# Two transformer layers on one core: attention's last masks, layer 1's first input sums, and where a product stands in two units

## The chip, the core and the metric

The kernel runs on one core of a Trainium2 chip. A core has five engines with a queue each: TensorE (matrix products; PE in the profile, its weight loads PEld), VectorE (DVE), ScalarE (ACT), GpSimd (POOL) and SyncE (SP), which starts transfers between the chip's large memory and SBUF, the on-chip memory of 128 partitions. TensorE writes its results to PSUM, which VectorE and ScalarE can read. Engines run on their own and wait for each other where a result or a buffer is needed; within one engine's queue the order is fixed when the program is compiled. The metric is the device time of one execution, in microseconds (us).

## What is computed

The input `x` has 2 sequences of 1024 rows of 512 numbers. Each of two layers normalises the rows and adds an "attention" branch and a feed-forward branch, both computed from the same normalised rows:

```python
xn = _layernorm(x, axis=-1)
x = x + _L0_attn_ref(xn, ...) + _L0_ffn_ref(xn, W1, W2, W3)
xn = _layernorm(x, axis=-1)
x = x + _L1_attn_ref(xn, W_qkv, b_qkv, W_out, b_out) + _L1_ffn_ref(xn, w_gate, w_up, w_down)
```

The change lies in layer 1. Its attention is causal, with 16 heads of 32 numbers, and its feed-forward keeps the two largest of each four hidden numbers:

```python
scores = jnp.einsum('bqhe,bkhe->bhqk', q, k) * scale
scores = jnp.where(causal[None, None], scores, -jnp.inf)
attn = jax.nn.softmax(scores, axis=-1)
...
h = jax.nn.silu(jnp.einsum('bsh,hi->bsi', x, w_gate)) * jnp.einsum('bsh,hi->bsi', x, w_up)
h_sparse = _sparsify_2to4(h)
return jnp.einsum('bsi,ih->bsh', h_sparse, w_down)
```

All of it is in float32.

## The kernel before

The 2048 rows are held as four blocks of 512 (`TT`), transposed: `xt1[i]` has the 512 features as 4 chunks of 128 partitions, and 512 columns, one for each row. Layer 0 runs first, then layer 1's attention, then layer 1's feed-forward.

**Attention** works through 8 units, each one sequence (of 2) and a group of 4 heads. A unit has two halves `j` of 512 queries. For a half, the key blocks `kt` of 128 come one after another: 4 for the first half, 8 for the second, so 12 steps a unit and 96 in all (`second`). A step's `weights` (line 1086) forms the scores of 4 heads on TensorE in two PSUM tiles, adds minus the row maxima to them by small products, and takes the exponential on ScalarE into two SBUF tiles `pt` (for `kt` 0 it is called `acc`). Where a key block lies on the diagonal (`kt >= 4 * j`), 128 of the columns hold entries that the mask forbids; a GpSimd `affine_select` (line 1117) sets these to zero. `gather` (line 1126), one step later, multiplies the values by `pt` into the bank `o` (line 1137) and adds `pt` to `acc` (line 1145), whose column sums are the softmax's denominators: `total` (line 1152) forms these on TensorE, `divide` (line 1164) takes reciprocals on VectorE and multiplies on GpSimd (line 1169). The additions of line 1145 go to GpSimd, and to VectorE once no maxima are left to be found:

```python
eng = nc.vector if per * u + 4 * j + kt + ahead >= len(second) else nc.gpsimd
```

`per` is 12, `ahead` 13 and `len(second)` 96, so this holds from step 83 on: the last step of unit 6 and all of unit 7.

The **order of the steps** is written out: a loop over steps `n` from -13 to 95 calls, in this order, `weights` of step n, what `put_mid` has for n, `gather` of step n-1, what `put_after` has, the search for maxima of step n+13, one part of a projection (`one_part`, chosen by due time), and what `put` has for n (`what_is_fixed`). `in_program_order` (line 48) ties each engine's instructions of this loop to that order. A last loop after it works off what is left: the output projections `project_out(8)` to `project_out(15)` (line 1176), each of two parts, 4 products that end in one VectorE addition to `x` (line 1179), with `total` and `divide` of the last half between them. The projections use two PSUM banks by turns. This last loop is not tied: the scheduler that compiles the program orders it.

**Layer 1's feed-forward** has 16 units; two make a group. A unit forms gate and up of a quarter of hidden features for two blocks of rows `x` and `y`, in `gate_up` (line 186), by Strassen's scheme as Winograd has it: seven products in place of eight, at the price of sums of the inputs (`tt`, four of them, by `combine_x` on VectorE, lines 156 to 161; one overwrites half of `y`) and of the weights (`s`, by `combine_w` on GpSimd, lines 169 to 172). Each product (`products`, line 175) is 4 matmuls of 128x128 by 512 columns, two for each half `m` of its pair of PSUM banks. Four of them add up in `pa`, two in `pc`, one stands alone in `pb`. After each product into `pa` that is not the last, ScalarE copies `pa` as it stands (lines 208, 216, 222), since the sum so far is wanted, and the next product into `pa` has to wait for that copy. `other_half` (line 201) is the product into `pb`, with a VectorE addition to `e[0]`. In units 1 to 15 it comes between the products with `s[1]` and `s[2]`; in unit 0 (`first`) it comes second, and the input sums are made by `hook(0)` right before it. From unit 2 on, the thinning (`sparsify`) and down products (`down_by_seven`) of the group before are put between the products, by the hooks. From line 1336 on the order is written out and tied as in attention.

Of the kernel before, what the change touches and what calls it, by code (L numbers as in the profile page):

```python
# [12 lines left out]
ALU = mybir.AluOpType  # L13
# [22 lines left out]
def two_layers(ctx: ExitStack, tc: tile.TileContext, t: dict, out: bass.AP):  # L36
# [135 lines left out]
        nc.gpsimd.tensor_sub(s[3], w1[:, :, 2:, :], s[1])  # L172
        return s

    def products(pair, a, x, start=False, stop=False):

        for m in range(2):
            for k in range(2):
                nc.tensor.matmul(  # L179
                    pair[:, m, :], a[:, m, k, :], x[:, k, :],  # L180
                    start=start and k == 0, stop=stop and k == 1, skip_group_check=True,
                )

    turns = 0

    def gate_up(pool, name, w1, w2, s, x, y, tt, h, hook, first=None):


        nonlocal turns
        e = [pool.tile([P, 2, TT], F32, tag=f"e{m}", name=f"e{m}_{name}") for m in range(1, 4)]  # L190

        pa, pc = (ps_pair(f"p{m}_{name}", (turns + m) % 3) for m in (0, 2))
        turns += 1

        def silu(m, i, gate):
            nc.scalar.activation(h(m, i), gate, AF.Silu)

        def up(m, i, lin):
            nc.vector.tensor_mul(h(m, i), h(m, i), lin)

        def other_half():
            pb = ps_pair(f"p1_{name}", turns % 3)
            products(pb, w1[:, :, 2:, :], x[:, 2:, :], start=True, stop=True)
            nc.vector.tensor_add(e[0], e[0], pb)
            hook(3)

        products(pa, w1[:, :, :2, :], x[:, :2, :], start=True)
        nc.scalar.copy(e[0], pa)
        hook(0)
        if first:  # L210
            other_half()
            y, tt = first()
        products(pc, s[0], tt[0], start=True)
        hook(1)
        products(pa, s[1], tt[1])
        nc.scalar.copy(e[1], pa)
        hook(2)
        if not first:
            other_half()
        products(pa, s[2], tt[2])  # L220

        nc.scalar.copy(e[2], pa)
        silu(0, 0, e[0][:, 0, :])
        nc.vector.tensor_add(e[2], e[2], pc)  # L224
        up(0, 0, e[0][:, 1, :])
        hook(4)
        silu(1, 1, e[2][:, 0, :])
        products(pa, w2[:, :, 2:, :], tt[3], stop=True)
        silu(1, 0, pa[:, 0, :])
        up(1, 1, e[2][:, 1, :])  # L230
        hook(5)
        up(1, 0, pa[:, 1, :])
        products(pc, s[3], y[:, 2:, :], stop=True)
        nc.vector.tensor_add(e[1], e[1], pc)
        hook(6)
        silu(0, 1, e[1][:, 0, :])
        up(0, 1, e[1][:, 1, :])
# [664 lines left out]
    in_program_order(start0)  # L902


    first_gu = {}
    with tc.tile_pool(name="b", bufs=1, reuse_waits="tile") as b:

        qk = {
# [13 lines left out]
        nc.gpsimd.affine_select(  # L922
            out=mask, in_=mask, compare_op=ALU.is_ge, fill=MASKED,
            base=0, pattern=[[-1, P]], channel_multiplier=1,
        )
        identb = b.tile([P, P], BF16, name="identb")
        nc.vector.tensor_copy(identb, ident)
# [146 lines left out]
        def shift_rows(u, half):  # L1074
# [8 lines left out]
            negs[u, half] = b.tile([P, TT], BF16, tag="neg", name=f"neg_{u}_{half}", bufs=4)  # L1083
            nc.vector.tensor_copy(negs[u, half], px[:, :NJ].rearrange("p t c -> p (t c)"))

        def weights(u, j, kt):

            q, k, neg = qk[u, 0], qk[u, 1], negs[u, j]
            name = f"{u}_{j}_{kt}"
            s = max(0, kt - 4 * j) * P  # L1090
            cols = slice(j * 512 + s, (j + 1) * 512)
            pair = [ps_wide(f"s_{name}_{p}") for p in range(2)]
            for h in range(4):
                rows = slice(h * HD, (h + 1) * HD)
                nc.tensor.matmul(  # L1095
                    pair[h // 2][:, h % 2, s:], k[rows, kt * P : (kt + 1) * P], q[rows, cols],
                    start=True, stop=False,
                )
            for h in range(4):
                rows = slice(h * HD, h * HD + 3)  # L1100
                nc.tensor.matmul(  # L1101
                    pair[h // 2][:, h % 2, s:], onesb[rows, :], neg[rows, s:],
                    start=False, stop=True,
                )
            got = []
            for p in range(2):

                if kt == 0:
                    pt = b.tile([P, 2, 512], F32, tag=f"acc{p}", name=f"acc_{name}_{p}", bufs=2)
                else:  # L1110
                    pt = b.tile([P, 2, 512], F32, tag="pt", name=f"pt_{name}_{p}", bufs=5)
                nc.scalar.activation(  # L1112
                    pt[:, :, s:], pair[p][:, :, s:], AF.Exp, scale=1.0 / math.sqrt(HD)
                )
                if kt >= 4 * j:
                    d = pt[:, :, s : s + P]
                    nc.gpsimd.affine_select(  # L1117
                        out=d, in_=d, compare_op=ALU.is_ge, fill=0.0,
                        base=0, pattern=[[0, 2], [1, P]], channel_multiplier=-1,
                    )  # L1120
                got.append(pt)
            return u, j, kt, s, got

        held, sums = {}, {}

        def gather(u, j, kt, s, pts):

            bb, hg = units[u]
            if kt == 0:
                held[u, j] = ps_bank(f"o_{u}_{j}", 0)  # L1130
                sums[u, j] = pts
            po = held[u, j]
            last = kt == 4 * j + 3
            v = vals[bb, kt // NJ, kt % NJ][:, hg * P : (hg + 1) * P]
# [4 lines left out]
                    start=(kt == 0), stop=last, tile_position=(0, h * HD),  # L1139
                )  # L1140
            if kt:

                eng = nc.vector if per * u + 4 * j + kt + ahead >= len(second) else nc.gpsimd
                for acc, pt in zip(sums[u, j], pts):
                    eng.tensor_add(acc[:, :, s:], acc[:, :, s:], pt[:, :, s:])  # L1145
            if last:
                att[u, j] = b.tile([P, 512], F32, tag="att", name=f"att_{u}_{j}", bufs=12)
# [4 lines left out]
        def total(u, j):  # L1152

            pw = ps_wide(f"w_{u}_{j}")[:, 0, :]
            for h in range(4):
                rows = slice(h * HD, (h + 1) * HD)
                nc.tensor.matmul(  # L1157
                    pw[rows, :], ones, sums[u, j][h // 2][:, h % 2, :],
                    start=True, stop=True, tile_position=(0, h * HD),
                )  # L1160
            inv[u, j] = b.tile([P, 512], F32, tag="inv", name=f"inv_{u}_{j}", bufs=1)
# [159 lines left out]
        n = len(second)  # L1321
        for m in range(QT, QT + NJ):
            rest.append((n, n + 9, project_out(m)))
        while rest or open_parts or fixed:
            one_part(n)
            what_is_fixed(n)
# [9 lines left out]
    with tc.tile_pool(name="c", bufs=1, reuse_waits="tile") as c_:  # L1336
# [167 lines left out]
                    if half == 0:  # L1504
                        tail.append((some_steps, n, 1, (3, 3, 3, 2)[2 * j + i]))

        tt, next_tt, second = None, None, None
        s_of = {}

        def unit_sums(n):  # L1510
# [2 lines left out]
        for n, (pb, g, half) in enumerate(units):  # L1513
# [11 lines left out]

            def hook(at):
                nonlocal tt, next_tt, second
                if n == at == 0:
                    tt, *make = combine_x(c_, x, y, "c0")
                    for f in make:  # L1530
                        f()
                for f, *args in between1.pop((n, at), ()):
                    f(*args)
                if at == 5 and n + 1 < len(units):
# [1 line left out]
                if at == 5 and n % 2 == 0 and n:  # L1536
                    load_down(n // 2)
                if at == 5 and n == len(units) // 2 - 1:
                    next_tt, first, second = combine_x(c_, xt1[2], xt1[3], "c1")
                    first()  # L1540

            gate_up(
                c_, f"c{n}", gu_w.pop((n, 0)), gu_w.pop((n, 1)), s_of.pop(n), x, y, tt,
                lambda m, i: h[:, 2 * half + m, i, :], hook,
                (lambda: (y, tt)) if n == 0 else None,
            )
            if n + 2 < len(units):
                load_gu(n + 2)
# [77 lines left out]
```

## Time and profile before

| what | us |
|---|---|
| median of 3 runs | 1851.51 |
| the three runs | 1851.51, 1851.51, 1860.42 |
| the profiled execution | 1851.87 |
| its span, first to last instruction | 1850.1 |
| layer 0 ends, attention's projections start | 676.45 |
| attention's last unit starts (scores of step 84) | 1177 |
| output projections 8 to 15 start | 1214.99 |
| layer 1's feed-forward starts | 1243.75 |

| engine | busy us | share of the span |
|---|---|---|
| TensorE | 1794.7 | 97% |
| VectorE | 1124.7 | 61% |
| GpSimd | 819.6 | 44% |
| ScalarE | 478.5 | 26% |

A timeline row is one engine's run of equal instructions: start, length, engine, line, operation, output and inputs by the program's names, shape and count, and in brackets the idle time before it with what ended it. Rows of a float32 product count two records for each matmul. In the table of stretches a number in brackets is a count of instructions. The granted TensorE clock is 0.996 over the run.

### The profile page before, as it was taken

The numbers are of one execution on the slowest core, as the hardware profiler recorded it, in microseconds if no ns is written. First come the engines' busy times: TensorE is split into PE (matmuls) and PEld (weight loads), VectorE is DVE, ScalarE is ACT, GpSimd is POOL, SyncE is SP. The second block draws the span as 40 slices with busy tenths as digits, with TensorE's granted clock in tenths as the row PEclk, the third lists the DMA queues.
The fourth block names the chain that finished last, engine by engine and source line by source line (L and its number), as shares of the span: only waits on it lengthen the run. The fifth ranks groups of instructions, "written<-read, shape, count | busy, mean of one in ns | idle before, by whom it ended". The sixth has DMA issues, their size and how long they took to land.

```text
span 1850.1 us, 18897 instructions
## 1 busy us (share of the span) xinstructions
PE 1794.7 (97%) x7348; PEld 916.4 (50%) x7348; DVE 1124.7 (61%) x1464; ACT 478.5 (26%) x683; POOL 819.6 (44%) x711
## 2 busy tenths in 40 slices
PE   7999999999999999999999999999999999999998
PEld 4446566555555564333333333333455555555553
DVE  3685444556544438566666566752867778668654
ACT  2322222222221102334343443412212212211210
POOL 4335364256542222467666766623243343334300
PEclk9999999999999999999999999999999999999999
DMA  6121111011101100000001000011011112201101
GB/s 228 35 80 34 35 35 46 23 46 35 35 23 34 35 18 12 1 12 13 12 1 35 12 13 1 24 46 42 27 57 34 46 32 72 80 23 57 34 1 46
DMA packets 29465, 68.12 MB, mean 37 GB/s; under 512 B 3392, under 2 KB 11584, under 8 KB 27840
## 3 DMA queue, kind: packets, MB, share of 16 engines
q1 hardware_dynamic: 28656, 66.61, 11.1%
q8 instruction: 59, 0.97, 0.2%
q10 hardware_dynamic: 720, 0.30, 0.1%
q14 instruction: 30, 0.25, 0.0%
HBM read 62.70 MB, written 4.19 MB: 36 GB/s over the span
## 4 chain that ended last, share of the span: by engine, by line
PE 87%; DVE 5%; POOL 3%; ACT 2%; issue 2%; DMA 0%; SPq 0%; ACTq 0%; POOLq 0%; DVEq 0%
PE p_a L179 20%; PE p_c L179 19%; PE d L297 19%; PE pq L990 6%; PE m L1042 4%; PE s L1095 4%; PE o L1137 3%; PE po L990 3%; PE pv L990 3%; PE dr L1454 2%; POOL acc L1145 2%; PE w L1157 1%; DVE tops L1050 1%; PE pp L579 1%; PE s L1101 1%
## 5 line engine op out<-in xcount | busy, mean ns | idle before, releaser
L315 POOL TENSOR_TENSOR x<-x,de 128x512 f32<-128x512 f32 x87 | 125.4, 1456 | 297.3 <-DVE x L310 162.5
L1145 POOL TENSOR_TENSOR acc<-acc,pt 128x1024 f32<-128x1024 f32 (+3 forms) x138 | 233.6, 1717 | 0.0
L1050 DVE TENSOR_REDUCE tops<-m 128x2 f32<-128x1024 f32 (+2 forms) x192 | 180.8, 955 | 49.1 <-PE m L1042 44.6
L310 DVE TENSOR_TENSOR x<-x,d 128x512 f32<-128x512 f32 x145 | 99.2, 684 | 151.5 <-PE d L297 150.5
L1112 ACT ACTIVATE pt<-s 128x1024 f32<-128x1024 f32 (+3 forms) x160 | 115.1, 766 | 180.1 <-PE s L1101 166.9
L297 PE MATMUL d<-td,h 128*128 128x256 f32 x592 | 139.9, 380 | 2.2 <-DVE h L272 2.2
L297 PEld LDWEIGHTS d<-td,h 128*128 128x128 f32 x592 | 112.2, 190 | 46.2 <-issue 29.2
L990 PE MATMUL pq<-xt,wqk 128*128 128x512 f32 x256 | 124.5, 614 | 0.8 <-ACT qk L1006 0.8
L179 PE MATMUL p_a<-t_a,s_a 128*128 128x512 f32 x256 | 116.9, 600 | 2.0 <-DVE t_a L156 2.0
L179 PE MATMUL p_c<-xt,s_c 128*128 128x512 f32 x256 | 115.2, 593 | 2.5 <-DVE e_c L224 1.4
L179 PE MATMUL p_a<-xt,w 128*128 128x512 f32 x256 | 116.8, 599 | 0.7 <-ACT xt L136 0.7
L179 PE MATMUL p_a<-xt,s_a 128*128 128x512 f32 x256 | 116.6, 598 | 0.0
L179 PE MATMUL p_c<-xt,gu 128*128 128x512 f32 x256 | 114.9, 592 | 0.0
L179 PE MATMUL p_c<-t_c,s_c 128*128 128x512 f32 x256 | 114.6, 592 | 0.0
L1049 DVE TENSOR_TENSOR m<-m,mask 128x256 f32<-128x256 f32 x128 | 54.7, 427 | 97.3 <-PE m L1042 92.7
L1042 PE MATMUL m<-qk,qk 32*128 32x512 f32 (+3 forms) x768 | 107.2, 533 | 3.7 <-ACT acc L1112 3.0
L1095 PE MATMUL s<-qk,qk 32*128 32x512 f32 (+3 forms) x768 | 93.5, 532 | 3.1 <-ACT pt L1112 2.2
L172 POOL TENSOR_TENSOR s_c<-gu,s_c 128x512 f32<-128x512 f32 x16 | 20.4, 1275 | 134.2 <-PE p_c L179 134.2
L1117 POOL TENSOR_SCALAR_AFFINE_SELECT pt<-pt 128x256 f32<-128x256 f32 x112 | 48.3, 448 | 69.5 <-ACT pt L1112 68.9
L990 PEld LDWEIGHTS pq<-xt,wqk 128*128 128x128 f32 x256 | 44.2, 189 | 65.9 <-issue 61.8
L179 PEld LDWEIGHTS p_a<-xt,s_a 128*128 128x128 f32 x256 | 47.2, 190 | 57.1 <-issue 56.7
L179 PEld LDWEIGHTS p_c<-xt,s_c 128*128 128x128 f32 x256 | 48.5, 190 | 54.2 <-issue 52.9
(240 smaller groups left out, 3044.6 us busy)
## 6 DMA issues: line engine op xcount, KB each, us to landing
w<-in_W SPq DMA_DIRECT2D x32, 512.0 KB, 3.6
gu<-in_gu SPq DMA_DIRECT2D x32, 512.0 KB, 3.5
wd<-in_down SPq DMA_DIRECT2D x8, 1024.0 KB, 4.8
x<-in_x SPq DMA_DIRECT2D x16, 256.0 KB, 4.3
w2h<-in_W2q SPq DMA_DIRECT2D x4, 1024.0 KB, 11.5
xr<-in_x SPq DMA_DIRECT2D x16, 256.0 KB, 2.7
wqk<-in_WqkvT SPq DMA_DIRECT2D x16, 256.0 KB, 3.1
out_x<-x SPq DMA_DIRECT2D x16, 256.0 KB, 2.0
```

Of the source, the lines that this page charges most:

```text
L179: nc.tensor.matmul(pair[:, m, :], a[:, m, k, :], x[:, k, :], start=start and k == 0, stop=stop and k == 1, skip_group_check=True,)
L297: nc.tensor.matmul(out_[:, j, :], lhs[:, q, j * P : (j + 1) * P], rhs[:, q], start=m in (0, 1, 3, 4) and j == q == 0, stop=j == q == 1, sk ...
L310: nc.vector.tensor_add(r, r, out_)
L315: nc.gpsimd.tensor_add(r, r, u2[half])
L990: nc.tensor.matmul(got[0], lhs(k), rhs(k), start=(k == 0), stop=(k == KC - 1))
L1042: nc.tensor.matmul(pair[h // 2][:, h % 2, :e], q[rows, qt * P : (qt + 1) * P], k[rows, c * 512 : c * 512 + e], start=True, stop=True,)
L1049: nc.vector.tensor_add(d, d, mask.unsqueeze(1).to_broadcast([P, 2, P]))
L1050: nc.vector.tensor_reduce(out=tops[u][:, c, qt, 2 * p : 2 * p + 2], in_=pair[p][:, :, :e], axis=mybir.AxisListType.X, op=ALU.max,)
L1095: nc.tensor.matmul(pair[h // 2][:, h % 2, s:], k[rows, kt * P : (kt + 1) * P], q[rows, cols], start=True, stop=False,)
L1112: nc.scalar.activation(pt[:, :, s:], pair[p][:, :, s:], AF.Exp, scale=1.0 / math.sqrt(HD))
L1137: nc.tensor.matmul(po[rows, s:], v[:, rows], pts[h // 2][:, h % 2, s:], start=(kt == 0), stop=last, tile_position=(0, h * HD),)
L1145: eng.tensor_add(acc[:, :, s:], acc[:, :, s:], pt[:, :, s:])
```

## The change

It has three parts.

*Masks.* The test by which line 1145 chooses its engine becomes a function, `idle_vector`. Where it holds for the step before (steps 84 to 95, all of unit 7), the mask on the diagonal is no longer a GpSimd `affine_select` but a VectorE minimum of `pt` with a new constant tile `allowed`, which is 1e30 where the mask allows and 0 elsewhere. `allowed` is made by two GpSimd instructions at the start of attention.

*Input sums.* A pool `sums`, opened before attention's pool and kept to the end, holds `t1`, `t2` and `t4`. The four sums for the first pair of blocks are put at `n + 5` and `n + 6` of the last loop of attention (`n` is 96), and unit 0's hook no longer makes them. The dictionary that was named `sums` is now `sums_of`.

*The product.* `products` takes the halves `m` that it is to do. In units 0 and 1 (`split`) `other_half` does `m = 0` between the products with `s[1]` and `s[2]`, and `m = 1`, with the addition to `e[0]` and hook 3, after the product with `s[2]` and its copy. Unit 0 has no special order any more.

```diff
+        pb = None
+
+        def other_half(of=(0, 1)):
+            nonlocal pb
+            if 0 in of:
+                pb = ps_pair(f"p1_{name}", turns % 3)
+            products(pb, w1[:, :, 2:, :], x[:, 2:, :], start=True, stop=True, of=of)
+            if 1 in of:
+                nc.vector.tensor_add(e[0], e[0], pb)
+                hook(3)
...
         if not first:
-            other_half()
+            other_half((0,) if split else (0, 1))
         products(pa, s[2], tt[2])
 
         nc.scalar.copy(e[2], pa)
+        if split:
+            other_half((1,))
         silu(0, 0, e[0][:, 0, :])
...
+    sums = ctx.enter_context(tc.tile_pool(name="sums", bufs=1))
     with tc.tile_pool(name="b", bufs=1, reuse_waits="tile") as b:
...
+        allowed = b.tile([P, P], F32, name="allowed")
+        nc.gpsimd.memset(allowed, -MASKED)
+        nc.gpsimd.affine_select(
+            out=allowed, in_=allowed, compare_op=ALU.is_ge, fill=0.0,
+            base=0, pattern=[[1, P]], channel_multiplier=-1,
+        )
...
+        def idle_vector(u, j, kt):
+
+            return per * u + 4 * j + kt + ahead >= len(second)
+
...
-                if kt >= 4 * j:
-                    d = pt[:, :, s : s + P]
+                d = pt[:, :, s : s + P]
+                if kt >= 4 * j and idle_vector(u, j, kt - 1):
+                    nc.vector.tensor_tensor(
+                        d, d, allowed.unsqueeze(1).to_broadcast([P, 2, P]), ALU.min
+                    )
+                elif kt >= 4 * j:
                     nc.gpsimd.affine_select(
...
-                eng = nc.vector if per * u + 4 * j + kt + ahead >= len(second) else nc.gpsimd
-                for acc, pt in zip(sums[u, j], pts):
+                eng = nc.vector if idle_vector(u, j, kt) else nc.gpsimd
+                for acc, pt in zip(sums_of[u, j], pts):
...
+        first_tt, *make = combine_x(sums, xt1[0], xt1[1], "c0")
+        for m, f in enumerate(make):
+            put(n + 5 + m, f)
         while rest or open_parts or fixed:
...
-        tt, next_tt, second = None, None, None
+        tt, next_tt, second = first_tt, None, None
...
-                if n == at == 0:
-                    tt, *make = combine_x(c_, x, y, "c0")
-                    for f in make:
-                        f()
...
-                    next_tt, first, second = combine_x(c_, xt1[2], xt1[3], "c1")
+                    next_tt, first, second = combine_x(sums, xt1[2], xt1[3], "c1")
...
-                lambda m, i: h[:, 2 * half + m, i, :], hook,
-                (lambda: (y, tt)) if n == 0 else None,
+                lambda m, i: h[:, 2 * half + m, i, :], hook, split=n < 2,
             )
```

## The prediction

> **What bounds the kernel now.** I read the page first. The busy times and the chain that ended last say that TensorE sets the end almost everywhere:
>
> ```profile
> PE 1794.7 (97%) x7348; PEld 916.4 (50%) x7348; DVE 1124.7 (61%) x1464; ACT 478.5 (26%) x683; POOL 819.6 (44%) x711
> ...
> PE 87%; DVE 5%; POOL 3%; ACT 2%; issue 2%; DMA 0%; SPq 0%; ACTq 0%; POOLq 0%; DVEq 0%
> ```
>
> So an edit is worth the TensorE idle time that it takes away or makes. I looked for that idle time in the timeline around the edited places: the last unit of attention (1176 to 1215 us), the last output projections (1215 to 1244) and the first two units of layer 1's feed-forward (1244 to 1299). TensorE's rows of layer 1, with the idle time in brackets:
>
> ```profile
> 1243.75 7.03 PE L179 MATMUL p_c<-xt,gu 128*128 128x512 f32 x16
> 1250.62 7.03 PE L179 MATMUL p_c<-t_c,s_c 128*128 128x512 f32 x16
> 1258.79 3.67 PE L179 MATMUL p_c<-xt,s_c 128*128 128x512 f32 x8 [1.15 <-issue]
> 1263.57 3.70 PE L179 MATMUL p_c<-t_c,gu 128*128 128x512 f32 x8 [1.10 <-ACT e_c L222]
> ...
> 1288.97 3.70 PE L179 MATMUL p_c<-t_c,gu 128*128 128x512 f32 x8 [1.10 <-ACT e_c L222]
> ```
>
> A product is 8 records, 3.43 us. TensorE stops three times in two units, each time because ScalarE is copying the accumulator (1.01 us) that the next product adds to: 1.15 + 1.10 + 1.10 = 3.35 us. Nothing stops it from 1215 to 1257.65, so the projections and the input sums cost it nothing today. In attention's last unit:
>
> ```profile
> 1181.89 1.59 PE L1137 MATMUL o<-acc,v 128*32 128x512 f32 x8 [1.26 <-POOL acc L1117]
> ...
> 1202.83 1.05 PE L1137 MATMUL o<-pt,v 128*32 128x512 f32 x4 [0.43 <-POOL pt L1117]
> ...
> 1204.17 1.05 PE L1137 MATMUL o<-pt,v 128*32 128x512 f32 x4 [0.29 <-POOL pt L1117]
> ...
> 1210.97 0.98 PE L1137 MATMUL o<-pt,v 128*32 128x256 f32 x8 [1.81 <-POOL pt L1117]
> ```
>
> With another 0.37 at 1186.1 the masks on GpSimd cost 1.26 + 0.37 + 0.43 + 0.29 + 1.81 = 4.16 us of idle TensorE. That is the most that moving them can give. But their new engine is the busiest after TensorE there, as the busy time by stretch shows (columns: stretch, its length, then PE, PEld, DVE, ACT, POOL):
>
> ```profile
> 1176.00:1190.00 14.00, 12.30 (x111) 4.48 (x113) 8.16 (x11) 7.24 (x15) 10.67 (x16) 1.00 0.13 53
> ...
> 1200.00:1215.00 15.00, 12.48 (x93) 3.99 (x87) 13.89 (x15) 5.78 (x9) 8.33 (x9) 1.00 0.32 119
> ```
>
> VectorE has 1.1 us free in the last 15. Its queue and GpSimd's there:
>
> ```profile
> 1201.35 2.50 DVE L1145 TENSOR_TENSOR acc<-acc,pt 128x1024 f32<-128x1024 f32 x2
> 1203.77 0.94 DVE L1167 RECIPROCAL inv<-inv 128x128 f32<-128x128 f32 x1
> 1204.63 2.41 DVE L1145 TENSOR_TENSOR acc<-acc,pt 128x1024 f32<-128x1024 f32 x2
> 1206.96 0.94 DVE L1167 RECIPROCAL inv<-inv 128x128 f32<-128x128 f32 x1
> 1207.83 2.82 DVE L1145 TENSOR_TENSOR acc<-acc,pt 128x768 f32<-128x768 f32 x2
> ```
>
> ```profile
> 1201.40 3.43 POOL L1117 TENSOR_SCALAR_AFFINE_SELECT pt<-pt 128x256 f32<-128x256 f32 x4 [7.31 <-ACT pt L1112]
> 1207.99 1.85 POOL L1169 TENSOR_TENSOR att<-att,inv 128x512 f32<-128x512 f32 x1 [3.16 <-DVE inv L1167]
> 1209.79 3.10 POOL L1117 TENSOR_SCALAR_AFFINE_SELECT pt<-pt 128x256 f32<-128x256 f32 x4
> ```
>
> The two engines hold each other up: a select is 0.40 us alone and 1.37 beside VectorE's additions (two of the four at 1201.40), the multiplication 1.27 alone and 1.85 there.
>
> **The change, part by part. 1: the product taken apart.** In units 0 and 1 half of `other_half` (1.72 us) comes before the product with `s[2]`, half after it. Each half lies over a copy: 1.01 us, started 0.2 after the product's end, is done 1.2 us after it, under 1.72. All three stops go: **-3.35 us**. What becomes late: the addition to `e[0]` now runs after the second half, 17.4 to 18.6 us into the unit, so the first silu follows at 18.6 and the addition to `e[2]` ends at 19.7. The last product needs that at 20.6: 0.9 us of slack. Unit 0's activation table load (1.28) fits between copy and silu. Vector work of unit 1 ends as late after its last product as before, so the two stops at 1313 to 1316 (0.29 + 1.50, the thinning steps on VectorE) stay. Bounds: 0 to -3.35; I take the whole, since the cover is longer than the copy in the same trace.
>
> **2: the input sums.** Four VectorE additions of 1.22 us (1244.56 to 1249.3) leave unit 0. Unit 0's second product now wants the first sum at 1247.2, where before `other_half` lay between. They go to the loop behind attention, two at a time, 2.4 us each. That loop is not held to the written order, and their inputs are old: the scheduler may put three of them as early as 677.5, where VectorE idles 15.06 us, and the in-place one into mid-attention. At the written place an addition of a projection (0.69) could wait 2.4 us; 2.4 + 0.69 = 3.1, and its bank is wanted after 3.43. So nothing either way; if all four come in a row, 4.9 + 0.7 - 3.4 = 2.2. I take **0**, bounds 0 and +2.2. No transfer moves with them. The 12 KB of `sums` push attention's tiles up, so that two of its first loads may wait for other tiles: the value weights on SP's queue (issued 608.9, landed 5.2 later, wanted at 711.1) and the bias on ScalarE's (653.8). Issued at 672, when layer 0's last GpSimd addition ends, the first lands 34 us early, and ScalarE is idle until 680.1 anyway: nothing. The tile `allowed` costs GpSimd 0.20 + 0.29 us near 672, before VectorE's mask is wanted at 692.6: nothing.
>
> **3: the masks.** Sixteen selects leave GpSimd, sixteen minima of 128x256 join VectorE, all in the last unit. Nearest row: the addition of 128x256 at 1190.3, 0.36 us, the next starting 0.28 after it; the addition of `mask` from PSUM is 0.43. I take 0.30 a piece, bounds 0.28 and 0.62 (such an addition beside GpSimd at 1181.5). Each minimum waits for its exponential on ScalarE, and the order puts it ahead of the step before's additions to `acc`: behind it queue these, the reciprocals, the copy of `neg`; TensorE waits for the minimum and, at the unit's end, for `acc`.
>
> I walked VectorE's queue through with these durations. First half (key steps 0 to 3): GpSimd's last additions run until 1181.3, the second minimum gets in after them, and the output product that started at 1181.89 starts at 1180.6 and is through 0.9 us earlier. But the additions of step 1, run at 1183.1 today, now stand behind the minima of step 2 and start at 1184.8; the copy of `neg` comes at 1188.1 against 1188.3, and TensorE's row that waits for it gains only 0.5. Second half (4 to 7), all 0.5 earlier at first: the reciprocals end at 1200.9, step 4's minima run at 1200.9 and, behind the second exponential, 1201.8; its product gains 1.7. Then come two additions (2.3), a reciprocal (0.9) and only then, at 1205.1, step 5's minima: that product starts 0.4 earlier than its 1205.91. Step 6's minima come behind two more additions and a reciprocal, and the second behind GpSimd's multiplication, at 1210.3; step 7's at 1212.2; the last additions end at 1214.5, and the addition that frees the first projection's bank at 1215.1 where it was 1214.6. TensorE restarts at about 1215.2 against 1214.99: **+0.2 us**. So the masks' 4.16 us of stops are not won: VectorE gets 8 x 0.30 = 2.4 us more in a stretch with 1.1 free, and wins back about 1 us of contention with the selects. Bounds: -4.16 (all stops gone) and, with 0.62 for each of those eight, 5.0 - 1.1 - 1.0 = +2.9.
>
> [...]
>
> **Sum.** -3.35 + 0 + 0.2 = -3.15 us. The profiled execution took 1851.87 (span 1850.1 and 1.77 around it): 1848.7. The median of the runs is 0.36 below it: **1848.4 us**, 0.17% faster. A measurement of this kernel tells about 0.5% (9.3 us) from no change, so this is no change.
>
> **Rivals.**
> - *The masks' stops go too.* VectorE's order leaves the minima early enough, and 4.16 us come back. For it: GpSimd is named in all five stops. Against: 13.89 of 15 us busy. 1851.5 - 3.35 - 4.16 = 1844.0.
> - *VectorE becomes the bound, and the kernel slower.* The place is steps 5 to 7 of the last unit, where each pair of minima stands behind up to 3.2 us of additions and reciprocal. At 0.62 a minimum the stretch grows by 2.9; it decides once the masks' part costs over 3.35, that is from 0.68 a piece or one more addition of 1.2 ahead of the last `acc`. At 0.9 a piece (half-way to the 1.47 of the contended one): 7.2 - 2.1 = 5.1, and 1851.5 - 3.35 + 5.1 = 1853.3. For it: contended additions of 0.62 to 1.47. Against: GpSimd has little left to contend with.
> - *The sums stand in the way.* All four in a row among the projections' additions: +2.2, 1850.6. For it: nothing fixes their place. Against: they are ready hundreds of us before.
> - *Taking apart does nothing*, because the copy or the silu now ends last: 1851.7. Against: 1.2 under 1.72.
>
> **How the numbers follow.** Chances: forecast 0.60 (own range 1846.5 to 1850), masks won 0.12, VectorE bound 0.12, sums 0.09, nothing 0.07. The range takes in the second case and reaches to the edge of the third: 1844.0 to 1853.0, with little over 0.1 left out. None of them reaches 9.3 us. Faster by over 0.5% would need more than all stops named here (7.5); slower by it would need the third case doubled, or the runs near 1860.42 that the kernel before has once in three. So 0.02, 0.94, 0.04.
>
> **What would show it.** Right: no idle TensorE before the products with `s[2]` and `tt[3]` in units 0 and 1, so that these two units take 3.35 us less; no GpSimd selects after 1179; VectorE over 14 of the last 15 us of attention, and output products waiting for VectorE's minima around steps 5 and 6 instead of GpSimd's selects; the first projection behind attention within 1 us of 1215.0. Wrong: that projection at 1212 or 1218; stops before the products with `s[0]` in unit 0, for a sum not made; additions of the projections late enough to hold a bank.

## The result and the profile after

| | median us | lowest to highest | executions | ratio to before, 95% interval |
|---|---|---|---|---|
| before | 1856.12 | 1851.19 to 1862.93 | 22 | |
| after | 1850.01 | 1847.47 to 1854.98 | 22 | 0.9972 [0.9964, 0.9981] |

The changed kernel is 0.28% faster by the means of its executions (1850.84 us against 1855.97), under the 0.5% that was called no change, and its median of 1850.01 us lies in the forecast range of 1844.0 to 1853.0 us. The forecast time, 1848.4, is 1.6 us too low although the forecast gain, 0.17%, is too small: it started from a median of three executions, 1851.51 us, and over 22 the kernel before has 1856.12. From there the same gain would have given 1853.0 us, 3.0 too high, so that the time itself was met this closely is luck in part.

The profiled execution of after took 1854.98 us (span 1853.3), more than before's profiled one (1851.87). One execution of each can't be compared as a whole, because TensorE's granted clock falls to a half for some stretches of 3.4 or 6.8 us, and their number and places differ: three in before's (from 28.7, 1813.9 and 1831.0 us), five in after's (from 31.8, 76.2, 1195.8, 1817.0 and 1834.1). Each execution has its mean clock on record, so below a *time at full clock* is given as well: the time less (1 - mean clock) x time. It is an estimate: the clock is on record to three digits, which is 0.9 us either way for one execution, and it takes off as much where TensorE waits as where it works. Before's 29 executions beside the first experiments spread by 2.4 us (standard deviation) and by 0.75 at full clock; they have a mean of 1844.4 us by it and after's 22 one of 1839.7; both have about 11 us taken off. One execution of an experiment below, the profiled one of neg_scalar, had a granted clock of 0.95 in every 20 us from 1180 to 1260 too and took 1913.16 us; it is left out of that kernel's ratio and times, and only its stops are read.

The page of after:

```profile
PE 1801.9 (97%) x7348; PEld 918.7 (50%) x7348; DVE 1136.3 (61%) x1480; ACT 479.1 (26%) x683; POOL 810.3 (44%) x697
...
PE 88%; DVE 6%; ACT 2%; POOL 2%; issue 2%; DMA 1%; ACTq 0%; DVEq 0%; POOLq 0%
```

VectorE has 16 instructions more, GpSimd 14 less (16 selects gone, two to make `allowed`). In the chain VectorE rose from 5% to 6% and GpSimd fell from 3% to 2%. TensorE's timeline in the first two units of the feed-forward (start, length, engine, line, operation, tiles, shape, count):

```profile
1261.33 1.88 PE L179 MATMUL p_c<-xt,gu 128*128 128x512 f32 x4
1263.04 3.60 PE L179 MATMUL p_c<-xt,s_c 128*128 128x512 f32 x8
1266.48 1.88 PE L179 MATMUL p_c<-xt,gu 128*128 128x512 f32 x4
1268.19 3.60 PE L179 MATMUL p_c<-t_c,gu 128*128 128x512 f32 x8
...
1275.06 3.60 PE L179 MATMUL p_c<-xt,gu 128*128 128x512 f32 x8
...
1287.08 3.60 PE L179 MATMUL p_c<-xt,s_c 128*128 128x512 f32 x8
...
1292.23 3.60 PE L179 MATMUL p_c<-t_c,gu 128*128 128x512 f32 x8
...
1299.09 3.60 PE L179 MATMUL p_c<-xt,gu 128*128 128x512 f32 x8
```

The product appears in two halves of 4 records, one on each side of the product with `s[2]`. Unit 1 runs from 1275.06 to 1299.09, where unit 2 starts. No row of the two units has an idle time in brackets: the three stops of 1.15, 1.10 and 1.10 us are gone. In attention's last unit they are not gone but have other causes (TensorE's timeline of after):

```profile
1185.52 1.81 PE L1162 MATMUL o<-acc,v 128*32 128x512 f32 x8 [0.42 <-ACT att L1172]
1193.72 0.40 PE L1122 MATMUL s<-neg,onesb 3*128 3x512 bf16 x4 [0.65 <-DVE neg L1101]
1213.42 1.17 PE L1162 MATMUL o<-pt,v 128*32 128x384 f32 x8 [1.60 <-DVE pt L1138]
1217.16 0.63 PE L1162 MATMUL o<-pt,v 128*32 128x256 f32 x4 [0.17 <-DVE pt L1138]
1218.57 0.63 PE L1162 MATMUL o<-pt,v 128*32 128x256 f32 x4 [0.79 <-DVE pt L1138]
1221.40 1.13 PE L179 MATMUL p_c<-xt,gu 128*128 128x512 f32 x2
1223.12 5.42 PE L1007 MATMUL po<-wout,att 128*128 128x512 f32 x12 [0.59 <-DVE x L1203]
```

The bracketed times add up to 4.22 us; before had 4.16. GpSimd's selects were named in all five before; now VectorE is named in five of six: the copy of `neg`, the minima (line 1138), the addition that frees a bank (line 1203). The row at 1221.40 was not expected: two records of unit 0's first product, placed ahead of the first output projection behind attention. The stretches that answer to the two shown of before (its length, then PE, PEld, DVE, ACT, POOL):

```profile
1180.50:1194.50 14.00, 12.86 (x117) 4.62 (x115) 10.10 (x19) 7.40 (x15) 6.05 (x8) 1.00 0.14 55
1208.12:1223.12 15.00, 11.85 (x86) 3.85 (x79) 14.51 (x22) 5.54 (x9) 1.27 (x1) 1.00 0.33 126
```

In the last 15 us ahead of that projection VectorE is busy for 14.51 (13.89 before) and GpSimd for 1.27 (8.33 before).

### The profile page after: what moved, and what is told of

It is laid out like the page before. It is cut to its first block, busy times and chain, and to the rows that moved or that the text cites. A ratio compares the mean times of both kernels' runs of the same rounds, so it can differ in the third digit from the quotient of the medians.

```text
span 1853.3 us, 18884 instructions
## 1 busy us (share of the span) xinstructions
PE 1801.9 (97%) x7348; PEld 918.7 (50%) x7348; DVE 1136.3 (61%) x1480; ACT 479.1 (26%) x683; POOL 810.3 (44%) x697
## 3 DMA queue, kind: packets, MB, share of 16 engines
q1 hardware_dynamic: 28656, 66.61, 10.9%
## 4 chain that ended last, share of the span: by engine, by line
PE 88%; DVE 6%; ACT 2%; POOL 2%; issue 2%; DMA 1%; ACTq 0%; DVEq 0%; POOLq 0%
PE p_a L179 20%; PE p_c L179 19%; PE d L305 19%; PE pq L1007 6%; PE m L1059 4%; PE s L1116 4%; PE o L1162 3%; PE po L1007 3%; PE pv L1007 3%; PE dr L1481 2%; POOL acc L1169 1%; DVE tops L1067 1%; PE s L1122 1%; PE w L1181 1%; ACT acc L1133 1%
## 5 line engine op out<-in xcount | busy, mean ns | idle before, releaser
L1059 PEld LDWEIGHTS m<-qk,qk 32*128 32x128 f32 x768 | 43.7, 183 | 64.4 <-issue 21.2
L179 PEld LDWEIGHTS p_a<-xt,w 128*128 128x128 f32 x256 | 49.6, 194 | 52.3 <-issue 49.7
```

Of the source, the lines that this page charges most:

```text
L179: nc.tensor.matmul(pair[:, m, :], a[:, m, k, :], x[:, k, :], start=start and k == 0, stop=stop and k == 1, skip_group_check=True,)
L1059: nc.tensor.matmul(pair[h // 2][:, h % 2, :e], q[rows, qt * P : (qt + 1) * P], k[rows, c * 512 : c * 512 + e], start=True, stop=True,)
```

## The experiments

They ran in three groups, each beside executions of the kernel before on the same chip. The columns: median, ratio to before with its 95% interval, mean time at full clock with its standard error, its difference to before's in the same group (1844.42 +- 0.14 for the first four rows, 1843.88 +- 0.13 for the next three, 1844.37 +- 0.32 for the last two), and the mean time taken off for the clock.

| kernel | median us | ratio | at full clock | difference | taken off |
|---|---|---|---|---|---|
| again | 1850.22 | 0.997 [0.9959, 0.9981] | 1839.94 +- 0.28 | -4.48 | 10.0 |
| masks_gpsimd | 1852.03 | 0.9986 [0.9975, 0.9997] | 1839.53 +- 0.33 | -4.89 | 13.3 |
| masks_only | 1853.57 | 0.9987 [0.9977, 0.9998] | 1844.10 +- 0.25 | -0.32 | 9.1 |
| not_apart | 1851.51 | 0.9979 [0.9966, 0.9992] | 1842.90 +- 0.26 | -1.52 | 8.8 |
| early_total | 1849.00 | 0.9969 [0.9959, 0.9978] | 1839.04 +- 0.37 | -4.84 | 9.9 |
| minima_twice | 1855.32 | 1.0006 [0.9992, 1.002] | 1843.20 +- 0.33 | -0.68 | 12.8 |
| sums_in_unit_0 | 1849.79 | 0.9973 [0.9962, 0.9983] | 1839.14 +- 0.30 | -4.74 | 10.9 |
| neg_scalar (3 executions) | 1848.21 | 0.9958 [0.9943, 0.9974] | 1839.34 +- 0.35 | -5.03 | 9.2 |
| combined | 1845.76 | 0.9946 [0.9932, 0.9959] | 1838.77 +- 0.68 | -5.60 | 8.1 |

### The change again

The changed kernel as it is, beside the next three.

> The changed kernel once more. Theory 1 (TensorE's stops decide: the taken-apart product gives back 3.35 us, the masks nothing): in a profile in which the clock is not halved inside attention, the way from step 83's scores to the start of unit 2 is 3.2 us shorter than before's 122.9 (less than 0.5 us either way), and the ratio is 0.998. Theory 2 (the masks' stops are won as well): 5 to 7.5 us shorter, ratio 0.9965. Theory 3 (stops decide 3 us, and the rest of the measured 0.28% is that the clock is halved less often): 3.2 us shorter as in theory 1, but the ratio stays near 0.997.

It took 1850.22 us, 0.30% under before, and its profile has the same stops in the same places as after's. By the two measures named above it does not decide between the three theories: its clock was halved for 6.8 us from 1192.9 on, inside attention's last unit, so that the way from step 83's scores to unit 2 (121.58 us) is not the one that was asked for, and the interval of its ratio takes in the 0.9965, the 0.997 and the 0.998. The experiments that follow take the change to pieces instead.

### Masks left on GpSimd

```diff
-                if kt >= 4 * j and idle_vector(u, j, kt - 1):
+                if False:
```

> The changed kernel with all masks left on GpSimd, so that only the sums and the taken-apart product are changed. Theory 1: the GpSimd stops of the last unit are back (about 4.2 us in sum) and VectorE's gone (4.2 us in the changed kernel), so step 83 to unit 2 is as long as in the changed kernel within 1 us, and the time too: ratio to before 0.998. Theory 2: 3 to 4 us longer than the changed kernel, ratio 1.000.

At full clock it gains all that the whole change gains, 4.9 +- 0.4 against 4.5 +- 0.3 us. The old stops at the end of attention are back (TensorE's timeline of masks_gpsimd):

```profile
1187.53 1.60 PE L1162 MATMUL o<-acc,v 128*32 128x512 f32 x8 [1.27 <-POOL acc L1142]
...
1216.63 0.99 PE L1162 MATMUL o<-pt,v 128*32 128x256 f32 x8 [1.81 <-POOL pt L1142]
```

From the first output projection behind attention to unit 2's first product it takes 76.82 us (1222.35 to 1299.18), where before took 80.95 (1214.99 to 1295.94): 4.13 us for three stops whose brackets add up to 3.35.

### Masks alone

The kernel before with `allowed` and the minima, nothing else.

```diff
+                d = pt[:, :, s : s + P]
+                if kt >= 4 * j and per * u + 4 * j + kt - 1 + ahead >= len(second):
+                    nc.vector.tensor_tensor(
+                        d, d, allowed.unsqueeze(1).to_broadcast([P, 2, P]), ALU.min
+                    )
+                elif kt >= 4 * j:
```

> The kernel before with the sixteen minima alone. Theory 1: from step 83 to the first projection behind attention (136.46 - 94.52 = 41.9 us before) nothing is won, +0.2 us within 1; stops of about 1.6 us at step 5's output product and 0.8 at step 6's; units 0 and 1 as before with three stops of 1.1; ratio 1.000. Theory 2: 4.2 us shorter, ratio 0.9978.

(The stretch from step 83's scores to that projection is 1214.99 - 1173.05 = 41.94 us before.) At full clock 0.3 +- 0.3 us are gained: nothing that can be told from none. The stops of the last unit are those of after to 0.02 us, and the three stops of the feed-forward are there unchanged, 1.15, 1.10 and 1.10. By the plain ratio it gains 0.13%, because less time was lost to the clock (9.1 against 11.2 us).

### Product not taken apart

```diff
-                lambda m, i: h[:, 2 * half + m, i, :], hook, split=n < 2,
+                lambda m, i: h[:, 2 * half + m, i, :], hook,
```

> The changed kernel with the product whole in units 0 and 1, between the products with s[1] and s[2]. All theories: one stop of 1.10 us in each of the two units, before the product with tt[3], so 2.2 us longer than the changed kernel; the stop of 1.15 before s[2] in unit 0 stays away, since the whole product now lies over that copy. If instead unit 0 and 1 are as long as in the changed kernel, taking apart is worth nothing.

In units 0 and 1 the product stands whole between those with `s[1]` and `s[2]`, as in the other units. Two stops are left (TensorE's timeline of not_apart):

```profile
1258.11 3.60 PE L179 MATMUL p_c<-xt,s_c 128*128 128x512 f32 x8
1262.81 3.70 PE L179 MATMUL p_c<-t_c,gu 128*128 128x512 f32 x8 [1.10 <-ACT e_c L228]
...
1280.08 3.60 PE L179 MATMUL p_c<-xt,gu 128*128 128x512 f32 x8
1283.51 3.60 PE L179 MATMUL p_c<-xt,s_c 128*128 128x512 f32 x8
1288.21 3.70 PE L179 MATMUL p_c<-t_c,gu 128*128 128x512 f32 x8 [1.10 <-ACT e_c L228]
```

It keeps 1.5 of the 4.5 us, so that halving the product brings 3.0 +- 0.4 (2.2 were expected, from the brackets). The rest is what the new order alone brings, which gives the copy ahead of unit 0's product with `s[2]` a whole product for a cover, and whatever the masks bring. The rows also give a stop's price. Products start 3.43 us apart (1280.08, 1283.51); over a stop it is 4.70 (1283.51, 1288.21). It costs 1.27, and 0.1 more behind it, where the next product starts 3.54 later (1262.81 to 1266.35): 1.37 to 1.38, not 1.10.

This profile has no half-clock stretch in attention or in the first units, so it also measures the masks alone:

```profile
1214.75 1.13 PE L179 MATMUL p_c<-xt,gu 128*128 128x512 f32 x2
1216.47 5.42 PE L1007 MATMUL po<-wout,att 128*128 128x512 f32 x12 [0.59 <-DVE x L1203]
```

From step 83's scores (1173.79) to the first projection behind attention (1216.47) it has 42.68 us, 0.73 more than before (41.95 by the records' unrounded times), and in them 0.86 of unit 0's first product (the two records at 1214.75, at a pitch of 0.43): -0.13 us.

### Half of the softmax's sums earlier

```diff
-                n = per * u + 8 * j + 7
+                n = per * u + 8 * j + 7 - 2 * (u == 7 and j == 0)
```

> The changed kernel with the denominators of unit 7's first half formed two steps earlier (at step 89 instead of 91), so that its four reciprocals (0.87 us apart) run while VectorE waits in steps 89 to 91 and no longer stand ahead of the minima of steps 4 to 6. If VectorE's queue is what takes the place of the GpSimd stops: the stop before step 5's output product falls from 1.6 us to under 0.8, that at step 6 from 0.96 to under 0.3, the one before the first projection goes, and from step 83's scores to unit 2 the kernel is 1.7 to 2.6 us shorter than the changed one where the clock is not halved. If the minima wait for their exponentials or for GpSimd instead, the stops stay.

The reciprocals for the last unit's first half come earlier, and the stops of its end become these (TensorE's timeline of early_total):

```profile
1208.27 1.05 PE L1162 MATMUL o<-pt,v 128*32 128x512 f32 x4 [0.73 <-DVE pt L1138]
1209.68 1.05 PE L1162 MATMUL o<-pt,v 128*32 128x512 f32 x4 [0.36 <-DVE pt L1138]
1212.29 1.17 PE L1162 MATMUL o<-pt,v 128*32 128x384 f32 x8 [0.80 <-DVE pt L1138]
...
1220.11 5.42 PE L1007 MATMUL po<-wout,att 128*128 128x512 f32 x12 [0.35 <-DVE x L1203]
```

The stop of 1.60 becomes 0.73 + 0.36 one step earlier and 0.80 at the old place, the two of step 6 go, and the last one is 0.35: 0.91 us less in all. VectorE is busy without a break from 1200.03 to 1220.4. At full clock this is 0.4 +- 0.5 us better than the change by the differences in the table, not the 1.7 to 2.6 that were expected: the stops did depend on where this work stood, but most of it was put elsewhere in a queue that stays full.

### Every minimum twice

```diff
-                    nc.vector.tensor_tensor(
-                        d, d, allowed.unsqueeze(1).to_broadcast([P, 2, P]), ALU.min
-                    )
+                    for _ in range(2):
+                        nc.vector.tensor_tensor(
+                            d, d, allowed.unsqueeze(1).to_broadcast([P, 2, P]), ALU.min
+                        )
```

> The changed kernel with each minimum done twice (the result is the same), so sixteen more VectorE instructions of about 0.3 us in the last unit. VectorE's queue as the bound: step 5's stop grows by 0.6 to 0.9 us (three more minima ahead of it), the first projection behind attention comes 2 to 2.6 us later, and the kernel at full clock takes 2 to 3 us longer than the changed one. If VectorE had room: under 0.7 us. The first half (steps 0 to 3) may add up to 0.6.

Four minima took 1.62 to 1.79 us where two took 0.69 to 0.92, and 3.05 and 2.56 where two that meet GpSimd took 2.22 and 1.78: some 0.9 more in each of the unit's eight steps with a diagonal, 3.4 us in its first half and 3.6 in its second. The kernel became 4.1 +- 0.4 us slower at full clock (against sums_in_unit_0 of the same group, whose attention is after's). TensorE's stops in that unit:

```profile
1182.90 1.78 PE L1163 MATMUL o<-acc,v 128*32 128x512 f32 x8 [1.27 <-DVE acc L1139]
1192.76 0.61 PE L1122 MATMUL s<-neg,onesb 3*128 3x512 bf16 x4 [1.49 <-DVE neg L1101]
1214.35 1.73 PE L1163 MATMUL o<-pt,v 128*32 128x384 f32 x8 [1.97 <-DVE pt L1139]
1219.96 0.63 PE L1163 MATMUL o<-pt,v 128*32 128x256 f32 x4 [1.48 <-DVE pt L1139]
1220.84 0.62 PE L1163 MATMUL o<-pt,v 128*32 128x256 f32 x4 [0.26 <-DVE pt L1139]
```

All wait for VectorE, and they add up to 6.47. So of 7.0 us more for VectorE some 4 come out in the time of the kernel: VectorE had no room, and it is what the end of attention waits for. That is more than the 2 to 3 us that were expected. The first half, for which up to 0.6 was allowed, has two stops that grew by 1.7 us together (0.42 to 1.27 and 0.65 to 1.49).

### Input sums back in unit 0

```diff
-        first_tt, *make = combine_x(sums, xt1[0], xt1[1], "c0")
-        for m, f in enumerate(make):
-            put(n + 5 + m, f)
...
+                tt, *make = combine_x(c_, x, y, "c0")
+                for f in make:
+                    f()
```

> The changed kernel with the four input sums made where they were, at the start of unit 0 on VectorE (1.22 us each), and the product still taken apart. If moving the sums is worth nothing by itself: the first sum is there 2 us after the projections' last product ends, before the second product asks for it at 3.4, there is no stop in units 0 and 1, and the time at full clock is that of the changed kernel within 0.5 us. If the move is what lets unit 0 run through, a stop of up to 1.3 us stands before the product with s[0].

The pool `sums` is gone too. No difference can be told: -4.74 +- 0.33 against -4.48 +- 0.31 us, and there is no stop in units 0 and 1. In this kernel VectorE makes the sums from 1249.66 to 1254.4, the product that reads the first (at 1251.43) starts without a wait, and the first lies beside unit 0's first product (from 1248.85).

### The copy of neg on ScalarE

```diff
-            nc.vector.tensor_copy(negs[u, half], px[:, :NJ].rearrange("p t c -> p (t c)"))
+            copy = nc.scalar.copy if (u, half) == (7, 1) else nc.vector.tensor_copy
+            copy(negs[u, half], px[:, :NJ].rearrange("p t c -> p (t c)"))
```

> The change whole, but the copy of neg for the last unit's second half goes to ScalarE, which is 26% busy, from VectorE. Theory (VectorE's queue is what the last unit of attention waits for): the 0.65 us stop of TensorE before the scores of step 88 goes, VectorE gets some 0.4 us free, and the first projection behind attention starts 0.5 to 1 us earlier after step 83's scores than in the changed kernel. Rival (the time is handed to the next wait on VectorE, the minima of step 5): the stop before step 5's output product grows from 1.60 to about 2.2 us, and the first projection starts within 0.2 us of where it did. By the sum of the whole run neither is over 0.06%, so the ratio to the kernel before stays at 0.997.

Two of the four stops in the last unit, from TensorE's timeline of its profiled execution, whose granted clock was 0.95 in that unit:

```profile
1223.62 1.73 PE L1163 MATMUL o<-acc,v 128*32 128x512 f32 x8 [0.39 <-ACT att L1173]
1247.81 1.19 PE L1163 MATMUL o<-pt,v 128*32 128x384 f32 x8 [1.56 <-DVE pt L1139]
```

The stop of 0.65 between these two is gone, and the next one did not grow (1.56 against 1.60, where the rival had 2.2). With the clock at 0.95 the lengths can't be set beside after's more closely than that. The three other executions are 0.6 +- 0.6 us below the change at full clock: of the expected size, and not told apart from none.

### Three shifts together

early_total, the copy of `neg` on ScalarE, and the first projection behind attention in the other bank:

```diff
         gather(*behind)
-        alone = 0
+        alone = 1
```

> The change whole, with three shifts that take work from VectorE's path at the end of attention: the sums for the softmax's denominators of the last unit's first half two steps earlier, the copy of neg of its second half on ScalarE, and the first output projection behind attention in the other of its two PSUM banks, so that it does not wait for the addition to x that empties the first. Theory (TensorE waits there only for VectorE's queue, so that each shift adds): of the 4.2 us of stops in the changed kernel's last unit about 2 us are left, and the time at an undisturbed clock is 1 to 2 us below the changed kernel's; ratio to the kernel before 0.996. Rival (VectorE is full to the end, so that only the additions that are left count): the stops move, 3 to 4 us of them stay, and the time is within 0.5 us of the changed kernel's; ratio 0.997.

TensorE's stops in the last unit of combined:

```profile
1184.54 1.81 PE L1163 MATMUL o<-acc,v 128*32 128x512 f32 x8 [0.42 <-ACT att L1173]
...
1206.60 1.05 PE L1163 MATMUL o<-pt,v 128*32 128x512 f32 x4 [1.43 <-DVE pt L1139]
1208.01 1.77 PE L1163 MATMUL o<-pt,v 128*32 128x512 f32 x4 [0.36 <-DVE pt L1139]
```

2.21 us of stops are left of 4.22, as the theory had it, and the projection starts without one. From step 83's scores (1176.53) to unit 2 (1294.19) it is 117.66 us, with one half-clock stretch in between; without such a stretch before took 122.89, and the change would take 118.6 (122.89 less 4.12 and 0.13, as measured; not_apart's 121.39 less two stops of 1.37 gives the same). So it is at least 1.0 us shorter, and the runs say 1.1 +- 0.8 at full clock. Its ratio to before, 0.9946 [0.9932, 0.9959], is the lowest of all. That it is faster than the change too rests on the trace more than on the runs: the change was not run in its group, and five executions leave 0.8 us of doubt.

### The kernel before again

> The kernel before, profiled a second time. It tells what one profiled execution can carry. If the stretches in which TensorE's granted clock falls to a half belong to places of the program, they lie at 28.7, 1813.9 and 1831.0 us as in the first profile, and the first output projection behind attention starts at 1214.99. If they belong to the execution, they lie elsewhere, and landmarks behind them shift by 1.7 us for each 3.4 us of half clock, while between two landmarks with none in between the distances stay within 0.1 us: 41.94 from step 83's scores (1173.05) to the first projection, 80.95 from there to unit 2 of the feed-forward (1295.94).

Its half-clock stretches lie at 30.6 (6.8 us), 75.0, 808.9, 1215.0, 1320.9 and 1819.2 (3.4 each), the first profile's at 28.7, 1813.9 and 1831.0. The ones near 30 and near 1814 (1819.2 less the 6.6 us by which this execution is late there) are in both; the other five are in one of the two only, so whether they come differs from execution to execution. Neither of the two answers holds alone, since the places at 75 and 1831 us come back in after's profile (76.2 and 1834.1). The same stretch of the program in the two profiles of before (columns as above; the last three are the granted clock, the share of the DMA engines and GB/s):

```profile
1215.00:1245.00 30.00, 30.00 (x74) 12.89 (x74) 9.14 (x13) 0.58 (x1) 6.21 (x5) 1.00 0.03 11
```

```profile
1215.00:1245.00 30.00, 30.00 (x80) 12.34 (x77) 9.89 (x15) 1.17 (x2) 7.39 (x7) 0.94 0.14 58
```

In the second the clock is 0.94 over 30 us: 3.4 us at a half. The first projection comes 43.62 us after step 83's scores in place of 41.95, 1.67 later for 3.4 us at half clock; from there to unit 2 it is 80.95 in both, to the hundredth.

## Why the prediction was right, and where it was not

**The class and the range** were right. The likeliest case held: the feed-forward's stops go, the masks' stops don't.

**Step 1, the product taken apart (-3.35).** The mechanism was right: all three stops went, and nothing came late behind them: the two stops in unit 2 are what they were, 0.30 and 1.51 us. The term was too small: it measured 4.12 us (from the first projection to unit 2 80.95 us became 75.97, and of the difference 0.86 is work that had been done earlier) and 4.13 in masks_gpsimd. The working took the idle time in the bracket for the price. A bracket is counted from the modelled end of the row before, 3.60 us after its start, while the next product could have started after 3.43; and 0.1 is lost at the restart. So 1.10 + 0.17 + 0.10 = 1.37 for a stop, and 3 x 0.27 = 0.8 was left out of the sum. Unit 1 shows it without any reckoning: seven products of 3.43 are 24.0 us, and the unit took 24.03 after, where before it took 25.40 with one stop (TensorE's timeline of before, the first products of units 1 and 2):

```profile
1270.54 3.60 PE L179 MATMUL p_c<-xt,gu 128*128 128x512 f32 x8
...
1295.94 3.60 PE L179 MATMUL p_c<-xt,gu 128*128 128x512 f32 x8
```

**Step 2, the input sums (0, bounds 0 and +2.2).** Right, and the place too: the scheduler made three of them right behind layer 0, and the one in place in mid-attention, beside additions on GpSimd (841.57 to 849.52), where it took 2.99 us in place of 1.22 (VectorE's timeline of after):

```profile
679.70 1.22 DVE L156 TENSOR_TENSOR t_c<-xt,xt 128x1024 f32<-128x1024 f32 x1
...
844.33 2.99 DVE L160 TENSOR_TENSOR xt<-xt 128x1024 f32<-128x1024 f32 x1
```

Nothing waited for either. That the move itself gains nothing that can be told (0.3 +- 0.5 us the other way) is shown by sums_in_unit_0.

**Step 3, the masks (+0.2, bounds -4.16 and +2.9).** It measured -0.13 us in not_apart, and 0.3 +- 0.3 of gain in masks_only. The reason given was right: the stops passed from GpSimd's selects to VectorE's queue. The walk can be followed in that queue (VectorE's timeline of not_apart, whose landmark before the unit, step 83's scores, stands 0.75 later than before's; the second fence is GpSimd's):

```profile
1180.27 2.22 DVE L1138 TENSOR_TENSOR acc<-acc,allowed 128x256 f32<-128x256 f32 x2 [1.38 <-ACT acc L1133]
...
1205.49 0.95 DVE L1191 RECIPROCAL inv<-inv 128x128 f32<-128x128 f32 x1
1206.35 0.69 DVE L1138 TENSOR_TENSOR pt<-pt,allowed 128x256 f32<-128x256 f32 x2
1206.96 2.35 DVE L1169 TENSOR_TENSOR acc<-acc,pt 128x1024 f32<-128x1024 f32 x2
1209.23 0.95 DVE L1191 RECIPROCAL inv<-inv 128x128 f32<-128x128 f32 x1
1210.09 1.78 DVE L1138 TENSOR_TENSOR pt<-pt,allowed 128x256 f32<-128x256 f32 x2
...
1215.74 0.68 DVE L1203 TENSOR_TENSOR x<-x,po 128x512 f32<-128x512 f32 x1
```

```profile
1179.52 2.69 POOL L1169 TENSOR_TENSOR acc<-acc,pt 128x512 f32<-128x512 f32 x2
...
1210.32 1.27 POOL L1193 TENSOR_TENSOR att<-att,inv 128x512 f32<-128x512 f32 x1 [15.02 <-DVE inv L1191]
```

With 0.75 taken off, step 5's minima run at 1205.6 (walk: 1205.1), step 6's end at 1211.1, the second held up by GpSimd's multiplication (the row at 1210.32) as the walk had it, and the addition that frees the bank ends at 1215.7 (walk: 1215.1). The walk was 0.5 us too early from step 5 on; already the copy of `neg` came at 1188.8 and not at 1188.1, behind two additions that took 1.29 together. That would have made +0.7, which is what TensorE's start shows (42.68 against 41.95 us). It became -0.13 because the scheduler filled part of the wait with 0.86 us of unit 0's first product, which the prediction did not have. Two misses, of 0.5 and 0.86, cancelled in part; that the size fits is luck to that extent.

**The two meetings with GpSimd** (1181.3 and 1210.3 in the walk). That a minimum waits there for the whole of GpSimd's instruction was an estimate, from one meeting in before: the first of the two additions at 1180.10 took 1.47 us beside GpSimd's, where one of the same size took 0.36 at 1190.3, and it ended 0.29 us after GpSimd's row (VectorE's row, then GpSimd's). It is also the 1.47 of the rival in which VectorE becomes the bound.

```profile
1180.10 2.01 DVE L1145 TENSOR_TENSOR acc<-acc,pt 128x256 f32<-128x256 f32 x2 [1.96 <-POOL acc L1145]
```

```profile
1178.78 2.50 POOL L1145 TENSOR_TENSOR acc<-acc,pt 128x512 f32<-128x512 f32 x2
```

The estimate held both times: a minimum that takes 0.36 us took 1.31 and 1.49 beside GpSimd in after, and in not_apart, at 1180.3 and 1210.3, the rows of two take 2.22 and 1.78, where two took 0.69 without GpSimd. Each of the two rows ends 0.28 us after GpSimd's row beside it (1182.49 against 1182.21, 1211.87 against 1211.59).

**The rivals.** That VectorE becomes the bound is half true: it is what the end of attention waits for, as minima_twice shows (7.0 us more of minima, 4.1 us slower), but the masks at their real size stay below the price at which it decides: the eight of the second half took 4.0 us in not_apart, 0.50 each, where the rival needed 0.68. The other rivals fell: the masks' stops were not won, the sums stand in nobody's way, and taking apart works.

**The sum.** 4.12 + 0.13 = 4.25 us are read from the traces, and the runs give 4.5 +- 0.3 at full clock. The measured 0.28% is 5.2 us; what is left over has no place in the program that could be shown, and the time lost to the clock varies by more than that between groups of executions. The same holds for the difference between again (0.997) and masks_gpsimd (0.9986): at full clock they are equal, and masks_gpsimd lost 13.3 us to the clock against 10.0. Whether masks on VectorE make such stretches rarer is open: masks_only and not_apart point that way (9.1 and 8.8), minima_twice does not (12.8).

## What to carry to other kernels

Moving work from the engine that the stops named to one that is busy for 13.9 of 15 us moved the stops here and did not remove them (4.16 us of them before, 4.22 after); walk through the new engine's queue before counting the gain, and look for what can leave that queue as well, which is where the next 1 us was. Price a stop of TensorE by the distance between starts with and without it, not by the idle time in the bracket, which here showed 1.10 of 1.37 us. Where a few microseconds matter, compare stretches between landmarks that have the same granted clock, and whole executions only by many runs.

## What the runs showed of the hardware

**The granted clock falls to a half in the middle of a busy kernel**, for 3.4 or 6.8 us at a time: three times in the profiled execution of before, five times in after's and six in before_again's (their places stand above), in the first two once more behind the last instruction (from 1851.4 and from 1854.5 us), and about 11 us of time lost in a mean one, 0.6%: more than this change brings. A stretch from about 30 us (28.7, 31.8, 30.6) and one near 1814 to 1819 (1813.9, 1817.0, 1819.2) are in all three; those near 75 and near 1831 are in two of them. A stretch of 3.4 us cost 1.67 us where it lay ahead of the first projection (43.62 us from step 83's scores in before_again in place of 41.95); 6.8 us over attention's last unit cost 3.0 and not 3.4 (step 83's scores to unit 2: 121.58 in again against 118.6 without one), where TensorE has 4.22 us of stops anyway. No long stop of TensorE goes ahead of the stretch at 1195.8 in after: its longest in the 20 us before is 0.65 us. What sets them off stays open.

**A stop's bracket undercounts its price**, by 0.27 us for each of these (4.70 us between starts in place of 3.43, and 0.10 more behind it, against a bracket of 1.10).

**A VectorE minimum of `pt` and `allowed` ended only behind the GpSimd instruction beside it**, both times that they met: 1.31 and 1.49 us in place of 0.36 in after, done 0.28 us after GpSimd's row in not_apart.

**In the loop that is not held to the written order, the scheduler filled waits with work from the next stage**: two records of the feed-forward stood ahead of the first projection in after, and six in minima_twice, where VectorE was later still.
